# Routing that chooses tiles by halves, and a combination whose residual is laid out by rows

## The chip, the cores and the metric

The kernel runs on one core of a Trainium2 chip. The metric is device microseconds for one launch, lower is better; where several runs are shown, their median is given. Times inside an execution are counted from its first instruction.

## The reference, cut to what matters

The whole program is two layers on an image x of shape (2, 256, 64, 64): layer 0 is area attention and a recurrence over tokens, layer 1 is a convolution block with a selective scan and then a mixture of experts. The change touches only the mixture of experts, which is the last stage:

```python
t = _to_tokens(x)                       # 2 * 4096 tokens of 256 channels
t = t + _L1_ffn_ref(_ln_t(t), gate_w, gate_b, W1, b1, W2, b2)
x = _from_tokens(t, x)

def _ln_t(v, eps=1e-5):                 # over the 256 channels of a token
    return (v - mean(v)) / sqrt(var(v) + eps)

def _L1_ffn_ref(x, ...):                # 8 experts, hidden size 512
    probs = softmax(xf @ gate_w + gate_b)
    top2_vals, top2_idx = top_k(probs, 2)
    cw = zeros((N, 8)); cw[token, top2_idx] += top2_vals
    for each expert e:
        acc += cw[:, e, None] * (gelu(xf @ W1[e] + b1[e]) @ W2[e] + b2[e])
    return acc
```

## The kernel before

The stage is the function experts, and it has three parts that follow one another: route, run_blocks, combine. Inside route and run_blocks the instructions of each engine stand in the order in which the code names them; the five engines (PE for matrix products and transposes, DVE, ACT, POOL, and SP, which here only issues DMAs) meet through semaphores.

**Route.** There are 64 tiles of 128 tokens, and the loop in normalise takes four at a time, so g runs over 16 groups. The image lies in SBUF with tokens on partitions (tok, which is the tile sh.x). For each group, turn (L1721) transposes the eight 128x128 blocks on PE into a PSUM tile "turned" (three buffers of two banks each) and ACT copies them to x_turned (x in this function), which has channels on partitions. measure (L1728) takes statistics of each tile on DVE, one or two instructions a tile; centre_gate (L1707) takes the mean out of the gate weights. Each four groups, gates (L1761) multiplies the gate weights with those 16 tiles of x_turned on PE and copies the product out on DVE, and turn_gates (L1774) transposes it back by PE and puts the logits in place. The PSUM tile of the product, by_expert, has one buffer. After the loop, root (L1733) makes the factor inv and the offset less of every token: six DVE operations, a square root on ACT (with a table load) and two more on DVE. Then the last product is turned, and scale (L1747) normalises each group, three tiles on ACT and one on POOL, and SP stores the rows to DRAM (rows), from four buffers xt. Last, choose (L1799) finds the two best experts of each token on DVE with operations over all 64 tiles at once (128x512), and ACT takes the exponents.

What follows in route is not changed: ranks of the tokens within their expert, the block numbers (wi, for the weights), then a table of which token stands where, made of products of one-hot tiles (high and named, low; L1925 to L1937). high is placed in memory that the xt buffers held, and so waits for their stores. The index lists xi and ri at L1951 end it.

**Run_blocks.** 68 blocks of 256 token slots run as a pipeline: POOL gathers rows and weights by indirect DMA, PE turns (L1976) and multiplies (L1988, L1998), ACT takes the Gelu, DVE copies (L1978) and adds the offset (L2006), and POOL puts the results in DRAM by indirect DMA (L2013). Where a block index over 68 is needed, a conditional part follows.

**Combine.** 16 groups of 512 tokens. SP loads both results of each token (y, two tiles of 512 KB, four buffers each), ACT scales the first by its weight (L2068), DVE multiplies and adds the second (L2069), in four steps k; PE transposes each step's two halves into po (L2073). Token 4p + k stands in row p of step k, so the four steps' columns interleave in the output. po holds them one step after another, and the views at L2081 to L2083 interleave while reading: DVE adds the residual of the first half of the channels (L2085), ACT copies the second half out of PSUM (L2087) and POOL adds its residual (L2088), since POOL's operand is not in PSUM. The residual is x_turned, where the tokens of one image row are 128 elements apart. POOL issues the store (L2089).

Of the kernel before, what the change touches and what calls it, by code (L numbers as in the profile page):

```python
# [18 lines left out]
P = 128  # L19
# [1598 lines left out]
def experts(tc, sh, ap, out, half, left):  # L1618
# [19 lines left out]
    with ExitStack() as ctx:  # L1638
# [5 lines left out]

        x = cp.tile([P, 2, WW, P], F32, name="x_turned")


        gate = cp.tile([P, 2, 32], F32, name="gate")
        nc.gpsimd.memset(gate, 0.0)
# [36 lines left out]

        ex = cp.tile([P, TILES, E], F32, name="ex")
        best, total = (cp.tile([P, TILES], F32, name=n) for n in ("best", "total"))
        held = ctx.enter_context(ExitStack())
        wp = held.enter_context(tc.tile_pool(name="e_w", bufs=3))  # L1690
        weights_of = {}
        full = [P, TILES, E]

        def over_experts(t):
            return t.unsqueeze(2).to_broadcast(full)

        def over_tiles(t):
            return t.unsqueeze(1).to_broadcast(full)

        def normalise(p2, logits):  # L1700

            with ExitStack() as own:
                ps = own.enter_context(tc.tile_pool(name="e_psum_n", bufs=3, space=PSUM))
                pg = own.enter_context(tc.tile_pool(name="e_psum_g", bufs=1, space=PSUM))
                pn = own.enter_context(tc.tile_pool(name="e_n", bufs=2))

                def centre_gate():  # L1707
                    of_gate = pg.tile([P, 512], F32, name="by_expert")[:, :32]
                    for c in range(2):
                        nc.tensor.matmul(of_gate, sh.mean_w, gate[:, c], start=c == 0, stop=c == 1)  # L1710
                    for c in range(2):
                        nc.vector.tensor_tensor(gate[:, c], gate[:, c], of_gate, ALU.subtract)
# [17 lines left out]
                        for c in (0, 1) if t in left else (1,):  # L1730
                            nc.vector.bn_stats(half[:, t, c], tok[:, t, c * P : c * P + P])

                def root():  # L1733

                    records = half.rearrange("p t c (i k) -> p t (c i) k", k=3)
                    means = records[:, :, :, 1]
                    nc.vector.tensor_reduce(mean, means, AX.X, ALU.add)
                    nc.vector.tensor_scalar(mean, mean, 0.25, None, ALU.mult)
                    nc.vector.tensor_tensor(away, means, mean.unsqueeze(2).to_broadcast([P, TILES, 4]), ALU.subtract)
                    nc.vector.tensor_tensor(away, away, away, ALU.mult)  # L1740
                    nc.vector.scalar_tensor_tensor(away, away, 64.0, records[:, :, :, 2], ALU.mult, ALU.add)
                    nc.vector.tensor_reduce(var, away, AX.X, ALU.add)
                    nc.scalar.activation(inv, var, AF.Sqrt, scale=1.0 / C, bias=sh.eps5)
                    nc.vector.reciprocal(inv, inv)
                    nc.vector.scalar_tensor_tensor(less, mean, -1.0, inv, ALU.mult, ALU.mult)
# [14 lines left out]

                def gates(q):  # L1761

                    pe = pg.tile([P, TB], F32, name="by_expert")
                    for c in range(2):
                        for j in range(4):
                            nc.tensor.matmul(
                                pe[32 * j : 32 * j + 32], gate[:, c], x[:, c, group(4 * q + j)],
                                start=c == 0, stop=c == 1, tile_position=(0, 32 * j),
                            )
                    mine = pn.tile([P, TB], F32, name="by_expert_s", bufs=1)  # L1770
                    nc.vector.tensor_copy(mine, pe)
                    return q, mine
# [8 lines left out]
                    )  # L1781


                waiting = None
                for g in range(TILES // K):
                    turn(g)
                    measure(g)
                    if g == 4:
                        centre_gate()
                    if g > 4 and g % 4 == 1:  # L1790
                        waiting = gates(g // 4 - 1)
                    if g > 4 and g % 4 == 2:
                        turn_gates(*waiting)
                root()
                turn_gates(*gates(3))
                for g in range(TILES // K):
                    scale(g)

        def choose(p1, logits):  # L1799

            pr, left = (p1.tile(full, F32, name=n) for n in ("pr", "left"))
            of = p1.tile([P, TILES], F32, name="of")
            nc.vector.tensor_tensor(pr, logits, over_experts(inv), ALU.mult)
            nc.vector.tensor_tensor(pr, pr, over_tiles(gate_b), ALU.add)
            nc.vector.tensor_reduce(of, pr, AX.X, ALU.max)
            nc.vector.tensor_tensor(pr, pr, over_experts(of), ALU.subtract)
            nc.scalar.activation(one, going[:, 0, 0:1], AF.Exp)
            nc.scalar.activation(ex, pr, AF.Exp)
            picks = [p1.tile(full, F32, name=f"pick{i}") for i in range(2)]
            for i, pick in enumerate(picks):  # L1810
                shifted = pr
                if i == 1:

                    shifted = left
                    nc.vector.scalar_tensor_tensor(left, picks[0], -3e38, pr, ALU.mult, ALU.add)
                    nc.vector.tensor_reduce(best, left, AX.X, ALU.max)
                    nc.vector.tensor_tensor(left, left, over_experts(best), ALU.subtract)
                nc.vector.scalar_tensor_tensor(pick, shifted, 0.0, over_tiles(rank), ALU.is_equal, ALU.mult)
                first = p1.tile([P, TILES], F32, name=f"first{i}")
                nc.vector.tensor_reduce(first, pick, AX.X, ALU.max)  # L1820
                nc.vector.tensor_tensor(pick, pick, over_experts(first), ALU.is_equal)
            nc.scalar.activation(best, best, AF.Exp)
            return picks, left

        def weigh():
            nc.vector.tensor_reduce(total, ex, AX.X, ALU.add)
# [17 lines left out]
        def route():  # L1844
            with ExitStack() as own:
# [2 lines left out]
                shared = p1.tile([P, NBLK * E], F32, name="logits")  # L1848
                logits = shared[:, : TILES * E].rearrange("p (t e) -> p t e", e=E)
                own.enter_context(tc.manual_schedule())  # L1850
                with tc.tile_pool(name="e_n2", bufs=4) as p2:
                    normalise(p2, logits)
                picks, left = choose(p1, logits)
                p4 = own.enter_context(tc.tile_pool(name="e_r4", bufs=2))
                ps = own.enter_context(tc.tile_pool(name="e_psum_r", bufs=1, space=PSUM))

# [99 lines left out]
        def run_blocks(lo, hi):  # L1956
            with ExitStack() as own:
# [70 lines left out]
                for i in range(lo, hi):  # L2028
# [18 lines left out]
                    below = i, act, now[1]  # L2047
                    if i == 8:
                        weigh()
                for _ in down(*below, None):  # L2050
                    pass

        def combine():
            with ExitStack() as own:
                p2 = own.enter_context(tc.tile_pool(name="e_c2", bufs=3))
                p4 = own.enter_context(tc.tile_pool(name="e_c4", bufs=4))
                ps = own.enter_context(tc.tile_pool(name="e_psum_c", bufs=3, space=PSUM))
                for g in range(T // TB):
                    b, n0 = g * TB // N, g * TB % N
                    y = [p4.tile([P, K, C], F32, name=f"y{i}") for i in range(2)]  # L2060
                    for i in range(2):
                        at = i * T + g * TB
                        got = nc.sync.dma_start(y[i], results[at : at + TB].rearrange("(p k) d -> p k d", k=K))
                        for put in puts:
                            tc.add_manual_dep(got.ins, put, landed, reason="all results first")
                    po = ps.tile([P, 2, TB], F32, name="po")
                    for k in range(K):
                        nc.scalar.activation(y[0][:, k], y[0][:, k], AF.Copy, scale=by_row[:, g, k, 0:1])  # L2068
                        nc.vector.scalar_tensor_tensor(  # L2069
                            y[1][:, k], y[1][:, k], by_row[:, g, k, 1:2], y[0][:, k], ALU.mult, ALU.add  # L2070
                        )
                        for c in range(2):
                            nc.tensor.transpose(  # L2073
                                po[:, c, k * P : k * P + P], y[1][:, k, c * P : c * P + P], sh.ident
                            )
                    cut = slice(n0, n0 + TB)
                    res = p2.tile([P, 2, TB], F32, name="res")
                    r0, r1 = HH * b + n0 // WW, HH * b + (n0 + TB) // WW
                    for c in range(2):

                        to = res[:, c].rearrange("p (r q k) -> p r q k", q=WW // K, k=K)  # L2081
                        turned = po[:, c].rearrange("p (k r q) -> p r q k", k=K, q=WW // K)
                        before = x[:, c, :, r0:r1].rearrange("p (q k) r -> p r q k", k=K)  # L2083
                        if c == 0:
                            nc.vector.tensor_tensor(to, turned, before, ALU.add)  # L2085
                        else:
                            nc.scalar.copy(to, turned)  # L2087
                            nc.gpsimd.tensor_tensor(to, to, before, ALU.add)  # L2088
                    nc.gpsimd.dma_start(out[b, :, cut].rearrange("(c p) n -> p c n", p=P), res)  # L2089

        route()
        run_blocks(0, OFTEN)
# [139 lines left out]
```

## Time and profile before

| | us |
|---|---|
| median of 3 runs | 3119.97 |
| lowest and highest of them | 3113.37, 3124.25 |
| the profiled execution, its own time | 3109.25 |
| its span, first to last instruction | 3107.5 |
| first instruction of the routing on PE (L1725) | at 2383.4 |
| first gather of rows for a block (L1834) | at 2481.4 |
| first load of the combination (L2063) | at 3018.7 |
| last store of the combination issued (L2089) | at 3101.5 |

The profile is one execution. Its rows have the engine, the line of the code, the tile written and the tiles read, the shape and the count; a row of the timeline begins with the start and the length in us (several instructions merged have one length), and in brackets how long the engine had stood idle and what released it. "PEclk" is the TensorE clock that was granted, as a share of full speed, and the DMA share is the mean busy share of the core's 16 DMA engines.

### The profile page before, as it was taken

What the parts mean: (1) busy time and instruction counts of PE and PEld (TensorE: products, weight loads), DVE (VectorE), ACT (ScalarE), POOL (GpSimd) and SP (SyncE); (2) the same over time, 40 slices, a digit from 0 to 9 for tenths busy, and PEclk for the clock granted to TensorE, in tenths of its full rate; (3) what the DMA queues carried; (4) which work ended last, traced back from release to release, by engine and by line L of the source; (5) the groups of instructions that cost most, each with busy time, mean ns of one, the idle gap of its engine ahead of it and who ended that gap; (6) DMA issues with size and microseconds to landing.
All of it is one profiled execution on the core that took longest, in us unless ns stands there. A gap on an engine that the chain in (4) does not pass through costs nothing. (4 is left out here: it accounts for less than half of the span.)

```text
span 3107.5 us, 45476 instructions
## 1 busy us (share of the span) xinstructions
PE 2745.6 (88%) x17734; PEld 1510.5 (49%) x17734; DVE 2246.1 (72%) x3331; ACT 1356.0 (44%) x2433; POOL 1355.6 (44%) x1034
## 2 busy tenths in 40 slices
PE   6988999999999999998779999987888399999974
PEld 1222222222222222222159999973445378888862
DVE  5699999999999999998966666779887811111127
ACT  2334444444444444444434455557663722222223
POOL 0343454544445454444731200018773256666644
PEclk8998999999999999999889999999999789999995
DMA  3000000000000000000023000005552456666657
GB/s 123 1 1 1 1 1 1 1 1 1 1 1 1 1 1 1 1 1 1 1 69 144 35 1 1 1 12 139 142 150 64 159 178 224 227 232 224 223 192 275
DMA packets 58579, 220.34 MB, mean 71 GB/s; under 512 B 14424, under 2 KB 15328, under 8 KB 48624
## 3 DMA queue, kind: packets, MB, share of 16 engines
q0 software_dynamic: 25504, 125.50, 11.4%
q1 hardware_dynamic: 31616, 87.56, 8.9%
q10 hardware_dynamic: 1232, 4.25, 0.4%
q8 instruction: 142, 2.33, 0.3%
q14 instruction: 85, 0.70, 0.1%
HBM read 173.30 MB, written 43.58 MB: 70 GB/s over the span
## 5 line engine op out<-in xcount | busy, mean ns | idle before, releaser
L577 POOL TENSOR_TENSOR ex<-ex,ex 128x1024 f32<-128x1024 f32 x255 | 636.3, 2497 | 768.6 <-PE ps L266 752.4
L271 DVE TENSOR_REDUCE nm<-ps 128x2 f32<-128x1024 f32 x512 | 601.3, 1219 | 129.4 <-PE ps L266 128.9
L359 ACT ACTIVATE ex<-ps 128x1024 f32<-128x1024 f32 x512 | 496.9, 1021 | 363.3 <-PE ps L352 343.9
L320 DVE SCALAR_TENSOR_TENSOR acc<-vh,w_pe,acc 128x1008 f32<-128x1008 f32 (+7 forms) x384 | 561.3, 1464 | 7.1
L266 PE MATMUL ps<-k,q 32*128 32x512 f32 x2048 | 352.4, 665 | 14.1 <-DVE nm L271 14.1
L1978 DVE COPY xt<-px 128x512 f32<-128x512 f32 x68 | 47.0, 692 | 417.0 <-PE px L1976 408.6
L352 PE MATMUL ps<-q,k 32*128 32x512 f32 x2048 | 304.8, 632 | 0.0
L1990 ACT ACTIVATE act<-ph,wt 128x256 f32<-128x256 f32 x272 | 128.8, 474 | 398.6 <-PE ph L1988 376.6
L365 PE MATMUL av_o<-ex,vt 128*32 128x512 f32 x2048 | 295.2, 645 | 4.5 <-ACT ex L359 4.3
L1988 PE MATMUL ph<-xt,wt 128*128 128x256 f32 x1088 | 293.5, 393 | 5.3 <-DVE xt L1978 3.6
L1998 PE MATMUL py<-wt,act 128*128 128x256 f32 x1088 | 280.0, 381 | 0.0
L266 PEld LDWEIGHTS ps<-k,q 32*128 32x128 f32 x2048 | 120.9, 191 | 231.6 <-issue 83.6
L347 PE MATMUL ps<-mx,ones_b 3*128 3x512 bf16 x1024 | 139.9, 392 | 102.0 <-DVE nm L271 101.3
L1988 PEld LDWEIGHTS ph<-xt,wt 128*128 128x128 f32 x1088 | 191.8, 192 | 68.2 <-DVE xt L1978 25.6
L773 PE MATMUL z<-xs,u 128*128 128x128 f32 x1872 | 223.6, 276 | 0.0
L773 PEld LDWEIGHTS z<-xs,u 128*128 128x128 f32 x1872 | 217.1, 193 | 0.0
L1998 PEld LDWEIGHTS py<-wt,act 128*128 128x128 f32 x1088 | 202.7, 191 | 25.1
L797 ACT ACTIVATE t<-z,bias 128x128 f32<-128x128 f32 x468 | 136.3, 362 | 145.4 <-PE z L785 145.3
L2013 POOL DMA_INDIRECT results<-y,ri x136 | 134.3, 988 | 145.6 <-DVE y L2006 103.9
L347 PEld LDWEIGHTS <-ones_b 3*128 3x128 bf16 x1024 | 36.4, 91 | 310.0 <-issue 307.3
L785 PE MATMUL z<-xs,v 128*128 128x128 f32 x1512 | 179.6, 275 | 0.0
L785 PEld LDWEIGHTS z<-xs,v 128*128 128x128 f32 x1512 | 174.2, 192 | 0.2 <-DVE xs L804 0.2
(409 smaller groups left out, 3930.8 us busy)
## 6 DMA issues: line engine op xcount, KB each, us to landing
cs<-c_rows SPq DMA_DIRECT2D x128, 256.0 KB
y<-results SPq DMA_DIRECT2D x32, 512.0 KB
x<-xrows SPq DMA_DIRECT2D x8, 1024.0 KB
rows<-xt SPq DMA_DIRECT2D x16, 512.0 KB
out_x<-res POOLq DMA_DIRECT2D x16, 512.0 KB
xrows<-xn SPq DMA_DIRECT2D x24, 256.0 KB
x<-in_x SPq DMA_DIRECT2D x4, 1024.0 KB
x<-in_x ACTq DMA_DIRECT2D x4, 1024.0 KB
```

The costliest lines, as they stand in the source:

```text
L266: mm = nc.tensor.matmul(tiles[h // 2][:, h % 2], qs[G, i // HM][head(h), i % HM * P : (i % HM + 1) * P], ks[G, n][head(h)], start=True, st ...
L271: nc.vector.tensor_reduce(nms[G][:, n, 2 * j : 2 * j + 2, i], tiles[j], AX.X, ALU.max, negate=True)
L320: nc.vector.scalar_tensor_tensor(part, vh[:, c, 2 + r0 + dy : 2 + r1 + dy, w0 + dx : w1 + dx], w_pe[:, c, k : k + 1], part, ALU.mult, ALU.add,
L347: nc.tensor.matmul(tiles[h // 2][:, h % 2], ones_b[at], mxs[G, n][at], start=True, stop=False, tile_position=(HD * h, 0),)
L352: nc.tensor.matmul(tiles[h // 2][:, h % 2], k[head(h), m % HM * P : (m % HM + 1) * P], qs[G, n][head(h)], start=False, stop=True, tile_pos ...
L359: nc.scalar.activation(exs[i], tiles[i], AF.Exp, scale=HD**-0.5)
L365: nc.tensor.matmul(to[head(h)], lhs, exs[h // 2][:, h % 2], start=first, stop=last, tile_position=(0, HD * h))
L577: add = nc.gpsimd.tensor_tensor(pair[0], *pair, ALU.add)
L773: nc.tensor.matmul(z[c][:, g, :m], u[:, k, c, g], xt[:, k], start=g == GATES[0] and k == 0, stop=False, skip_group_check=True,)
L785: nc.tensor.matmul(z[c][:, g, :m], v[:, k, c, g], h[:, k], start=False, stop=k == 1, skip_group_check=True,)
L1988: nc.tensor.matmul(ph[:, hc], wt[:, at : at + P], xt[:, c], start=c == 0, stop=c == 1)
L1998: nc.tensor.matmul(py[:, j], act[:, hc, j * P : j * P + P], wt[:, at : at + C], start=hc == 0, stop=hc == NH - 1,)
```

## The change

Routing: the statistics of groups 0 to 7 are all taken at group 4 and those of groups 8 to 15 at group 5, followed at once by the first part of root. The gate product has two PSUM buffers and its copy out is a function of its own (take_gates); the turned tile has two buffers instead of three. The square root, and the choice for tiles 0 to 31, stand at group 10; from group 11 on, one group of scaling follows each turn. The last two gate products are turned after the loop, and the choice for tiles 32 to 63 comes after all scalings. The operations of choose are the same, on 128x256 each, so there are twice as many; the exponents stay whole.

Blocks: in blocks 12 to 43 DVE copies one piece of 128x512 of x_turned into the memory of sh.x, which nothing reads any more, in the order of the tokens (lay_out).

Combination: the transposes write po with a step of four elements, so that po is in the order of the tokens; DVE adds the residual of both halves in one instruction of 128x1024, ACT's copy and POOL's addition are gone, and y has five buffers. In the last group the halves are added and stored one by one, the second by SP.

```diff
...
+        placed = sh.x.rearrange("p c b n -> p (c b n)").rearrange("p (c m w) -> p c m w", c=2, w=WW)
...
-                ps = own.enter_context(tc.tile_pool(name="e_psum_n", bufs=3, space=PSUM))
+                ps = own.enter_context(tc.tile_pool(name="e_psum_n", bufs=2, space=PSUM))
...
-                def root():
+                def root_in():
...
                     nc.vector.tensor_reduce(var, away, AX.X, ALU.add)
+
+                def root_out():
+
                     nc.scalar.activation(inv, var, AF.Sqrt, scale=1.0 / C, bias=sh.eps5)
...
                 def gates(q):
 
-                    pe = pg.tile([P, TB], F32, name="by_expert")
+                    pe = pg.tile([P, TB], F32, name="by_expert", bufs=2)
...
+                    return q, pe
+
+                def take_gates(q, pe):
                     mine = pn.tile([P, TB], F32, name="by_expert_s", bufs=1)
                     nc.vector.tensor_copy(mine, pe)
                     return q, mine
...
                 for g in range(TILES // K):
                     turn(g)
-                    measure(g)
                     if g == 4:
+                        for i in range(8):
+                            measure(i)
                         centre_gate()
                     if g > 4 and g % 4 == 1:
                         waiting = gates(g // 4 - 1)
-                    if g > 4 and g % 4 == 2:
+                        if g < 12:
+                            waiting = take_gates(*waiting)
+                    if g == 5:
+                        for i in range(8, TILES // K):
+                            measure(i)
+                        root_in()
+                    if 4 < g < 12 and g % 4 == 2:
                         turn_gates(*waiting)
-                root()
-                turn_gates(*gates(3))
-                for g in range(TILES // K):
+                    if g == 10:
+                        root_out()
+                        halves[0]()
+                    if g > 10:
+                        scale(g - 11)
+                last = gates(3)
+                turn_gates(*take_gates(*waiting))
+                turn_gates(*take_gates(*last))
+                for g in range(5, TILES // K):
                     scale(g)
-
-        def choose(p1, logits):
...
+                halves[1]()
+
+        def choose(p1, logits, half):
+
+            at = slice(half * TILES // 2, (half + 1) * TILES // 2)
+            pr, left, *picks = (t[:, at] for t in p1)
...
+                    if 12 <= i < 12 + 2 * T // TB:
+                        lay_out(*divmod(i - 12, 2))
...
+        def lay_out(j, c):
+
+            rows_ = slice(j * TB // WW, (j + 1) * TB // WW)
+            nc.vector.tensor_copy(placed[:, c, rows_], x[:, c, :, rows_].rearrange("p w m -> p m w"))
...
-                p4 = own.enter_context(tc.tile_pool(name="e_c4", bufs=4))
+                p4 = own.enter_context(tc.tile_pool(name="e_c4", bufs=5))
...
-                    po = ps.tile([P, 2, TB], F32, name="po")
+
+                    po = ps.tile([P, 2, P, K], F32, name="po")
...
-                            nc.tensor.transpose(
-                                po[:, c, k * P : k * P + P], y[1][:, k, c * P : c * P + P], sh.ident
-                            )
+                            nc.tensor.transpose(po[:, c, :, k], y[1][:, k, c * P : c * P + P], sh.ident)
                     cut = slice(n0, n0 + TB)
                     res = p2.tile([P, 2, TB], F32, name="res")
-                    r0, r1 = HH * b + n0 // WW, HH * b + (n0 + TB) // WW
-                    for c in range(2):
-
-                        to = res[:, c].rearrange("p (r q k) -> p r q k", q=WW // K, k=K)
-                        turned = po[:, c].rearrange("p (k r q) -> p r q k", k=K, q=WW // K)
-                        before = x[:, c, :, r0:r1].rearrange("p (q k) r -> p r q k", k=K)
-                        if c == 0:
-                            nc.vector.tensor_tensor(to, turned, before, ALU.add)
-                        else:
-                            nc.scalar.copy(to, turned)
-                            nc.gpsimd.tensor_tensor(to, to, before, ALU.add)
-                    nc.gpsimd.dma_start(out[b, :, cut].rearrange("(c p) n -> p c n", p=P), res)
+                    before = placed[:, :, g * TB // WW : (g + 1) * TB // WW]
+                    parts = [slice(0, 2)] if g < T // TB - 1 else [slice(0, 1), slice(1, 2)]
+                    for eng, cs in zip((nc.gpsimd, nc.sync), parts):
+                        nc.vector.tensor_tensor(
+                            res[:, cs], po[:, cs].rearrange("p c m k -> p c (m k)"),
+                            before[:, cs].rearrange("p c m w -> p c (m w)"), ALU.add,
+                        )
+                        eng.dma_start(out[b, :, cut].rearrange("(c p) n -> p c n", p=P)[:, cs], res[:, cs])
```

## The prediction

> **What bounds the kernel now.** I read the page first, then the timeline of the two stages that the diff touches, then one stage's groups, and last the DMA shares by stretch. The page gives the stage map: DVE, ACT and DMA in 40 slices of 77.7 us.
>
> ```profile
> span 3107.5 us, 45476 instructions
> DVE  5699999999999999998966666779887811111127
> PEclk8998999999999999999889999999999789999995
> DMA  3000000000000000000023000005552456666657
> ```
>
> Routing lies in the 31st and 32nd slice, where DVE reads 7 and 8 (2383 to 2482 us); the run of 1 after it is the expert blocks, bound by PE; the last slice, where DVE is 7 and the granted clock 0.5, is the combination (3018.7 to 3107.5 us). The timeline of the combination shows its first group and a later one:
>
> ```profile
> 3023.87 1.67 DVE L2069 SCALAR_TENSOR_TENSOR y<-y,by_row,y 128x256 f32<-128x256 f32 x4 [10.23 <-DMA y<-results]
> 3026.41 1.01 DVE L2085 TENSOR_TENSOR res<-po,x_turned 128x512 f32<-128x512 f32 x1 [0.87 <-PE po L2073]
> ...
> 3045.42 1.01 DVE L2085 TENSOR_TENSOR res<-po,x_turned 128x512 f32<-128x512 f32 x1 [0.87 <-issue]
> 3046.34 2.99 DVE L2069 SCALAR_TENSOR_TENSOR y<-y,by_row,y 128x256 f32<-128x256 f32 x4
> ...
> 3047.14 1.52 POOL L2088 TENSOR_TENSOR res<-res,x_turned 128x512 f32<-128x512 f32 x1 [2.25 <-ACT res L2087]
> ...
> 3050.20 1.01 DVE L2085 TENSOR_TENSOR res<-po,x_turned 128x512 f32<-128x512 f32 x1 [0.87 <-issue]
> ```
>
> A group lasts 4.78 us (3045.42 to 3050.20). DVE is in it all the time: four multiply-adds, 0.87 waiting for PE's last transposes, one addition. The four take 1.67 in the first group, where POOL is idle, and 2.99 later; POOL's own addition of 1.52 starts inside them. The tile view of y shows where the 1.3 go: one in four is stretched.
>
> ```profile
> L2069 DVE SCALAR_TENSOR_TENSOR y<-y,by_row,y x64: 471/479/1811, 3023.9 to 3096.7; 128x256 f32<-128x256 f32 x64
> ```
>
> The page's chain of waits blames POOL; I read it as POOL lengthening DVE's round. Next the transfers of the stage: the column before the last is the DMA share, the last GB/s.
>
> ```profile
> 3030.00:3050.00 20.00, 9.91 (x36) 5.46 (x36) 15.97 (x21) 8.34 (x19) 9.75 (x9) 0.50 0.98 378
> 3070.00:3084.00 14.00, 6.69 (x24) 3.65 (x24) 11.39 (x16) 6.56 (x15) 6.72 (x6) 0.50 0.90 335
> 3084.00:3107.00 23.00, 6.69 (x24) 3.65 (x24) 12.40 (x16) 5.95 (x13) 8.96 (x8) 0.50 0.28 109
> ```
>
> The engines are full only while loads still run; the last 23 us carry stores alone at 0.28. Transfers are the next bound, not this one. Last the routing's timeline:
>
> ```profile
> 2413.71 0.35 ACT L1743 ACTIVATE inv<-var,eps 128x64 f32<-128x64 f32 x1
> 2414.94 23.69 ACT L1756 ACTIVATE xt<-x,less,inv 128x256 f32<-128x256 f32 x48 [0.88 <-DVE less L1745]
> 2416.40 0.29 DVE L1778 COPY logits<-by_token 128x128 f32<-128x128 f32 x1 [0.89 <-PE by_token L1777]
> 2426.93 0.69 DVE L1859 TENSOR_TENSOR both<-pick,pick 128x512 bf16<-128x512 f32 x1
> 2441.83 0.76 DVE L1925 TENSOR_TENSOR high<-place,hi 128x576 bf16<-128x576 bf16 x1 [1.68 <-DMA rows<-xt]
> ```
>
> Two chains meet at L1925: the normalised rows (root, 48 ACT scalings, their stores), and DVE's choice (logits, thirteen operations, the ranks), which is ready 1.68 us earlier. So routing ends on the row stores, with DVE 1.68 behind.
>
> **The change part by part: combination.** ACT's copy, POOL's addition and one of two DVE additions go; DVE adds both halves at once, 128x1024, from a PSUM tile and a residual that both lie in order. Durations:
> - The multiply-adds fall back to the first group's 1.67, as no POOL instruction reads SBUF beside them.
> - PE is then what the addition waits for: from the first multiply-add to the addition 3026.41 - 3023.87 = 2.54.
> - The addition: nearest rows are L1497 (DVE, 128x1024 out of PSUM) at 1.23 and L2006 at 0.69 for 512. I take 1.23; the next instruction starts 0.08 before its end, as now (3045.42 + 1.01 against 3046.34).
>
> So 2.54 + 1.15 = 3.69 a group. First multiply-add to last addition is 74.1 now (3023.9 to 3098.0); then 15 x 3.69 + 2.54 = 57.9: 16.2 less. The tail from the last addition to the end is 9.5 now (addition 1.0, ACT 0.6, POOL 1.5, gaps, then 6.0 from the issue at 3101.5). Then: two half additions 1.4, 0.1, and some 5.7 from SP's issue (0.32 instead of POOL's 0.73): 7.2, so 2.3 less. Combination: -18.5.
>
> Does the DMA allow it? 16 groups move 16 x 1.573 = 25.2 MB; at 390 GB/s (the best slice, 3020 to 3030) 4.0 us a group, above 3.69. But loads run ahead: at 390 GB/s the first five groups' loads (1.05 MB each) take 13.5 us without a store between them, one group more than the four buffers of now allow, and this lead of some three groups pays 16 x 0.3 = 5 us. So it just fits; the rival below is that it doesn't.
>
> **A rule against this step.** The transposes now write PSUM with a step of four elements, 16 bytes. The row: L1308 already writes with a step of two, and its 64-column matmul takes 216 ns where L1184's, written in order, takes 218. The Trainium skill, "SBUF — State Buffer", section "Door 1: The DMA port swizzle", says in its note on cachelines that PSUM has 8-byte lines and that any PSUM pattern out of order slows matmuls significantly. L1308 already meets a new line at each element, and pays nothing; so I add 0. By the rule it turns round. A group is 1.77 + 9x, with x the 0.213 us from one transpose to the next: 0.54 until the first (3024.41 in the trace), seven steps, 2x for the last, 0.08 to the addition, 1.15. With x doubled it is 5.6, and the combination gets 15 x 5.6 + 4.5 - 74.1 - 2.3 = 12 us longer instead of 18.5 shorter.
>
> **The residual's layout.** 32 DVE copies of 128x512, one a block in blocks 12 to 43, read with a step of 512 bytes. No row is the same: from 0.42 (L1740, 256 elements, if it runs at two a clock) to 1.52 (POOL on this very view); I take 1.0, like L2085. Each stands behind y's addition on DVE, and the next DVE instruction (the px copy L1978) comes after 5.99 us of idling in every block: 0 on the path. If that gap were gone, 32 us. POOL's queue of puts and gathers is the other neighbour; the trace has no SBUF-to-SBUF copy beside its indirect DMAs. The Trainium skill, same page, section "SBUF: two separate sides", says that such an fp32 copy keeps GpSimd from writing descriptors while it runs. By the trace POOL idles 1.47 before each block's put; by the rule the put starts later by the copy's length, and up to 1.5 that idling takes it. 0 by either.
>
> **Routing.** On DVE now: 32 measures of 0.198 from 2385.45 to 2391.8, gate centring to 2392.1 (0.9 later than before), idle 2.0 for the first gate product (1.92 on PE), its copy to 2394.8, then 46 measures and six root operations in one run: 9.1 + 2.7, to 2406.7 (before 2412.4). Behind that run stand the logits copy and the second gate copy; behind the latter PE's transposes of it, and behind these, on PE, the turns of groups 11 to 15. Before, all 16 turns were copied at 2408.9. Now PE stands from about 2401.5 to 2407.7. The root comes at 2408.4, 5.7 earlier, but ACT then alternates a copy (0.95) with three scalings (1.48): group 15's copy ends near 2410.2 + 4 x 2.43 = 2420. The 48 scalings end at 2437.7 against 2438.6, so the row stores gain only 1. The first half's choice (thirteen at 0.42 to 0.54, 6.3 with gaps) ends at 2415.7, hidden. But the last gate product needs group 15: it ends at 2422.0, and then transposes, copies, transposes and copy follow one another (2.65), then the second choice 6.3 and the sum 0.75: 2431.7 against 2427.6. DVE's slack of 1.68 is eaten and 2.4 remain. The two halves cost 12.6 for 10.2, which is part of this. A second bank for gate products saves nothing while ACT's copy decides; two turned buffers instead of three cost nothing, since ACT paces them. And the clock: it was granted 1.0 until 2415, 0.73 to 2417 and 0.5 after, some 5 us after PE fell idle, and needed as long to come back at 2383. PE's stand may cost that again; the last products then last up to 3.84. So +2 to +6.5; I take +3.5.
>
> **Sum.** -18.5 + 3.5 + 0 = -15.0. The profiled execution took 3109.25 (span 3107.5 and 1.75 around it): 3094.3. It lies 10.7 under the median of the runs shown, 3119.97; from that, 3105.0.
>
> **The rivals.**
> 1. Routing is no loss (0.17): if the clock holds and ACT's copies come between DVE's waits more kindly, the row stores still end it, 1 earlier. For: DVE has 1.68 to spare. Against: the last product behind ACT. -19: 3101.
> 2. Transfers become the bound (0.15): at the 378 GB/s of 3030 to 3050, 4.16 a group. 74.1 - (15 x 4.16 + 2.54) + 2.3 = 11.5 gained, 3.5 lost: 3112. For: share 0.98. Against: 0.28 at the end.
> 3. Slower (0.04): PSUM's step bounds PE. From x = 0.38 on, with 27.2 + 144x - 74.1 - 2.3 + 3.5, the total is over 0.3% slower; with x doubled it is 12 + 3.5 more: 3135.5. L1308 speaks against it.
> 4. It doesn't do what it says (0.04): the stretch of 1.3 is not POOL's and stays: 2.98 + 0.87 + 1.15 = 5.0 a group, +4 in all: 3124. Against: the first group.
>
> **How the numbers follow.** Likeliest (0.60): 3105. A measurement of this kernel can tell about 0.3%, 9.4 us; the three runs shown differ by 10.9. With some 4 us of spread around each case, the main one is faster by more than that at 0.92, rival 1 nearly always, rival 2 at 0.36, the others never: 0.77. Rival 3 and the far tails are slower: 0.06. Same: 0.17. Range: the routing's bounds, rival 1 below, rival 2 above, and the runs' spread: 3095 to 3115.
>
> **What would show it.** Right: no L2069 over 0.5 us, L2115 (the new addition) near 1.23 and 3.7 apart, no POOL addition, 128x128 transposes still 0.42; the copies beside blocks of unchanged 7.55; PE idle before by_token around 2402 to 2407, and high starting at 2444 to 2448 with no wait for the row stores. Wrong: transposes longer than 0.42, DVE waiting for y loads in the combination, or high before 2442.

## The result, and the profile after

The changed kernel takes 3100.19 us (median of 10 runs, 3094.54 to 3109.60); ten runs of the kernel before beside it have a median of 3118.18. The ratio is 0.9947, with a 95% interval of 0.9933 to 0.9961: faster by 12.2 to 20.9 us, by 18.0 between the medians. The forecast was 3105.0 with a range of 3095 to 3115.

The profiled execution of the changed kernel took 3105.5 us, only 3.75 less than that of before, and this pair of numbers would mislead. The two traces are best compared by stage, each from an instruction that both kernels have:

| stage | before | after | difference |
|---|---|---|---|
| start to the first turn of the routing (unchanged code) | 2383.5 | 2399.6 | +16.1 |
| routing, from the first turn to the first `high` | 58.4 | 62.0 | +3.6 |
| table and expert blocks, from `high` to the first y load | 576.9 | 571.7 | -5.2 |
| combination, from the first y load to the end | 88.7 | 70.3 | -18.4 |
| span | 3107.5 | 3103.5 | -4.0 |

The first and the third row are not the change's. In twelve executions of the kernels of this study the unchanged first stage ends anywhere between 2381.0 and 2399.6; most of the 16.1 arises in the attention before 1320 us. The third row comes from single late blocks among blocks of 7.55 us. In before the block after the second is 2.9 late, and one near the end is 2.4 late; in after neither is. The first lateness goes with the TensorE clock: in before full clock is granted again 62.9 after `high`, in after 56.5 after it, and in the ten executions where it comes at 61.1 to 62.9 this block is 2.0 to 2.9 late, in the two where it comes at 56.2 and 56.5 it is not. Why the second comes is not shown. Either turns up with the old routing and with the new. The two changed stages repeat better: the changed routing lies between 61.2 and 62.0 in five executions, the changed combination between 69.6 and 70.5 in six. So the experiments below are read by stages.

The page of after, the same rows as before:

```profile
span 3103.5 us, 45453 instructions
...
DVE  5689999999989999998966666779888832222115
...
PEclk8998999999999999999979999998999789999995
DMA  3000000000000000000012200004553336666658
```

In the last slice DVE has gone from 7 to 5 and the DMA engines from 7 to 8: less work for DVE, and the same bytes in a shorter time. The timeline of the combination after, one group and the start of the next:

```profile
3045.71 1.66 DVE L2105 SCALAR_TENSOR_TENSOR y<-y,by_row,y 128x256 f32<-128x256 f32 x4
...
3046.24 1.97 PE L2109 MATMUL po<-ident,y 128*128 128x128 f32 x8 [1.71 <-DVE y L2105]
3048.25 1.23 DVE L2115 TENSOR_TENSOR res<-po,x 128x1024 f32<-128x1024 f32 x1 [0.87 <-PE po L2109]
3049.39 1.66 DVE L2105 SCALAR_TENSOR_TENSOR y<-y,by_row,y 128x256 f32<-128x256 f32 x4
...
3051.94 1.23 DVE L2115 TENSOR_TENSOR res<-po,x 128x1024 f32<-128x1024 f32 x1 [0.89 <-PE po L2109]
```

A group lasts 3051.94 - 3048.25 = 3.69 us, and the four multiply-adds 1.66. The tile view of y (minimum, median and maximum in ns) shows that none is stretched any more:

```profile
L2105 DVE SCALAR_TENSOR_TENSOR y<-y,by_row,y x64: 474/479/486, 3038.3 to 3095.7; 128x256 f32<-128x256 f32 x64
```

The transfers in the middle of the stage (the third column from the right is the granted clock, then come the DMA share and GB/s):

```profile
3057.00:3069.00 12.00, 6.38 (x27) 4.68 (x28) 9.32 (x18) 5.18 (x13) 2.90 (x4) 0.50 1.03 419
```

The engines are full, at 419 GB/s. DVE waits for a load inside the stage only once, for 0.45.

The routing after, on PE, DVE and ACT:

```profile
2416.60 1.09 PE L1729 MATMUL turned<-ident,x 128*128 128x128 f32 x8
2423.51 1.12 PE L1787 MATMUL by_token<-ident,by_expert_s 128*128 128x128 f32 x4 [5.81 <-DVE by_expert_s L1781]
2424.42 5.17 PE L1729 MATMUL turned<-ident,x 128*128 128x128 f32 x24
...
2435.91 1.00 ACT L1730 COPY x_turned<-turned 128x1024 f32<-128x1024 f32 x1
...
2439.49 0.29 DVE L1788 COPY logits<-by_token 128x128 f32<-128x128 f32 x1 [7.04 <-PE by_token L1787]
...
2448.12 0.77 DVE L1887 TENSOR_TENSOR both<-pick,pick 128x512 bf16<-128x512 f32 x1
...
2461.56 0.81 DVE L1953 TENSOR_TENSOR high<-place,hi 128x576 bf16<-128x576 bf16 x1 [0.23 <-issue]
```

PE stands for 5.81 us behind the copy of the second gate product. The turns that follow take 5.17 for 24, against 2.78 before, since the granted clock had fallen to 0.5. The row of before, and the stretch of after with its clock (third column from the right):

```profile
2400.91 2.78 PE L1725 MATMUL turned<-ident,x 128*128 128x128 f32 x24
```

```profile
2423.00:2427.00 4.00, 3.49 (x17) 3.49 (x18) 2.69 (x7) 1.99 (x3) 1.15 (x2) 0.50 0.02 4
```

ACT's last copy starts at 2435.91, DVE waits 7.04 for the last but one gate product, and `high` no longer waits for the row stores: DVE's own chain now ends the routing.

### The profile page after: what moved, and what is told of

Same layout as the page of the kernel before. It is cut to its first block, busy times and chain, and to the rows that moved or that the text cites. A ratio compares the mean times of both kernels' runs of the same rounds, so it can differ in the third digit from the quotient of the medians.

```text
span 3103.5 us, 45453 instructions
## 1 busy us (share of the span) xinstructions
PE 2755.1 (89%) x17734; PEld 1515.8 (49%) x17734; DVE 2253.2 (73%) x3377; ACT 1348.7 (43%) x2417; POOL 1332.3 (43%) x1018
## 5 line engine op out<-in xcount | busy, mean ns | idle before, releaser
L2006 DVE COPY xt<-px 128x512 f32<-128x512 f32 x68 | 47.0, 692 | 395.1 <-PE px L2004 395.1
L2016 PEld LDWEIGHTS ph<-xt,wt 128*128 128x128 f32 x1088 | 190.4, 191 | 65.8 <-DVE xt L2006 23.5
```

What stands on the lines that cost most here:

```text
L2016: nc.tensor.matmul(ph[:, hc], wt[:, at : at + P], xt[:, c], start=c == 0, stop=c == 1)
```

## The experiments

All times that follow are us from the profile of the kernel named; "both", "copy of group 15" and "high" are starts counted from the first turn. Each stage length is that of one execution. The measured stages together:

| kernel | both | copy of group 15 | high | combination |
|---|---|---|---|---|
| before | 43.5 | 24.5 | 58.4 | 88.7 |
| after | 48.5 | 36.3 | 62.0 | 70.3 |
| combination alone | 42.3 | 23.3 | 57.2 | 70.5 |
| routing alone | 48.0 | 36.1 | 61.5 | 89.2 |
| no GpSimd addition | 42.5 | 23.5 | 57.4 | 77.0 |
| GpSimd addition beside | 48.0 | 36.1 | 61.3 | 83.7 |
| po in order | 48.0 | 36.1 | 61.2 | 71.4 |
| four y buffers | 48.0 | 36.0 | 61.5 | 69.6 |
| scalings behind | 44.8 | 32.7 | 60.5 | 69.6 |
| second copy earlier | 49.0 | 37.1 | 62.5 | 69.8 |
| gates turned late | 44.1 | 24.8 | 57.5 | 70.5 |
| root before the last copies | 41.1 | 25.3 | 54.6 | 70.3 |

**The two parts alone.** The kernel before with the new `combine` (its five y buffers too), `lay_out` and its calls; the calls are

```diff
...
+                    if 12 <= i < 12 + 2 * T // TB:
+                        lay_out(*divmod(i - 12, 2))
...
```

> The kernel before with the new combination, the layout copies and five y buffers, and with the old routing. Stage lengths in the profile: routing from the first turn to high 58.4 before and 62.0 after; combination from the first y load to the end 88.8 and 70.3. Theory (the two parts are independent; the combination gains 18.5 and the routing loses 3.6): routing 58.4, combination 70.3, the time before less 18.5, so a ratio of 0.994. Rival (the routing only loses because the layout or the fifth buffer moves something, or the combination gains from an earlier end of the routing): routing 60 or more, or a combination of 72 or more.

The median is 3096.09 us against 3116.51, a ratio of 0.9935 (0.9923 to 0.9948). The routing is 57.2 and the combination 70.5: the gain needs nothing of the new routing. And the changed routing with the old combination, without the layout copies:

> The changed routing with the old combination and without the layout copies. Theory: routing 62.0, combination 88.8, so 3.6 more than before, with the stretched multiply-adds (one in four at 1.81) back. Rival (part of the routing's 3.6 is scatter between executions): routing 58 to 60. The blocks between high and the first y load were 576.9 before and 571.7 after: if that belongs to the routing, they take some 572 here and some 577 with the old routing; if it is scatter (the clock's return in the first two blocks, and one block that is 2.4 late), it follows neither.

`high` comes at 61.5 and the combination takes 89.2, with multiply-adds of up to 1.81 again. The blocks take 574.2 here and 573.9 with the combination alone, so the 5.2 of the third stage follow neither part. Five executions with the changed routing as it is (after, routing alone, GpSimd addition beside, po in order, four y buffers) have `high` at 61.2 to 62.0, mean 61.5; three with the old one at 57.2 to 58.4, mean 57.6. The routing's loss is 3.9.

**GpSimd's addition taken away, and put back.** (GpSimd is POOL in the rows, VectorE is DVE, ScalarE is ACT, TensorE is PE.) First it goes from the kernel before, and ScalarE's copy with it; VectorE adds both halves:

```diff
-                        if c == 0:
-                            nc.vector.tensor_tensor(to, turned, before, ALU.add)
-                        else:
-                            nc.scalar.copy(to, turned)
-                            nc.gpsimd.tensor_tensor(to, to, before, ALU.add)
+                        nc.vector.tensor_tensor(to, turned, before, ALU.add)
```

> The kernel before, whose combination adds both halves of a group on VectorE (two additions of 128x512 as they stand); ScalarE's copy and GpSimd's addition are gone, everything else stays. Theory (GpSimd's addition is what stretches one multiply-add in four to 1.81): no multiply-add over 0.5, four in 1.67; a group is 1.67 + 0.87 + 2 x 0.93 = 4.40 against 4.78, and the combination 88.8 less 15 x 0.38 less 1 to 2 at the end: 81 to 82. Rival (the stretch comes from the y loads or from ScalarE): four multiply-adds still take 2.99, a group 2.99 + 0.87 + 1.86 = 5.7, and the combination about 102.

The combination takes 77.0, less than expected. Its timeline, of an early and of a later group:

```profile
3031.67 1.97 PE L2073 MATMUL po<-ident,y 128*128 128x128 f32 x8 [2.43 <-DVE y L2069]
...
3033.68 1.96 DVE L2084 TENSOR_TENSOR res<-po,x_turned 128x512 f32<-128x512 f32 x2 [0.87 <-PE po L2073]
...
3052.71 1.66 DVE L2069 SCALAR_TENSOR_TENSOR y<-y,by_row,y 128x256 f32<-128x256 f32 x4
...
3053.24 1.97 PE L2073 MATMUL po<-ident,y 128*128 128x128 f32 x8 [2.01 <-DVE y L2069]
3054.82 1.94 DVE L2084 TENSOR_TENSOR res<-po,x_turned 128x512 f32<-128x512 f32 x2 [0.45 <-PE po L2073]
...
3056.70 1.65 DVE L2069 SCALAR_TENSOR_TENSOR y<-y,by_row,y 128x256 f32<-128x256 f32 x4
```

The multiply-adds are at 1.66 though the additions still are the old ones, so the stretch came from what was taken away, GpSimd's addition or ScalarE's copy; the next run tells which. The first four groups take 4.40, as expected. From the fifth on a group takes some 3.98: the first addition then waits 0.45 for PE and not 0.87. In the early group it starts when all eight transposes are done (3031.67 + 1.97 = 3033.64), in the later one 0.39 before that (3053.24 + 1.97 = 3055.21). Eleven groups shorter by 0.42 are 4.6, which is what the forecast of 81 to 82 lacked; why only the later groups need not wait for all eight is not shown. Of the combination's 18.4, the move of GpSimd's addition to VectorE brings 11.7. The rest, 77.0 - 70.3 = 6.7, comes with the residual and PSUM in order, one addition a group, and the last group stored in halves; these were not taken apart.

Then the converse: the changed kernel, with a GpSimd addition of the old size in each group, on which nothing waits (`idle` is a tile of its own).

```diff
...
+                idle = p2.tile([P, TB], F32, name="idle", bufs=1)
...
+                    nc.gpsimd.tensor_tensor(
+                        idle.rearrange("p (r q k) -> p r q k", q=WW // K, k=K),
+                        idle.rearrange("p (r q k) -> p r q k", q=WW // K, k=K),
+                        x[:, 1, :, r0:r1].rearrange("p (q k) r -> p r q k", k=K), ALU.add,
+                    )
...
```

> The changed kernel with GpSimd adding, once a group, the old strided 128x512 view of the residual to a tile of its own that nobody reads: an addition of the old size beside the multiply-adds, on which nothing waits. Theory (it is this that stretches one multiply-add in four): one in four at 1.8, a group 2.99 + 0.87 + 1.15 = 5.0 against 3.69, the combination 70.3 + 15 x 1.3 = 90. Rival (the stretch needs the old chain, in which GpSimd's addition waited on ScalarE's copy): multiply-adds at 0.48, a combination of 70 to 72.

It takes 83.7, neither 90 nor 70. The order of GpSimd's work is why: with nothing to wait for, its sixteen additions run in one row from the stage's start.

```profile
3027.94 26.20 POOL L2113 TENSOR_TENSOR idle<-idle,x_turned 128x512 f32<-128x512 f32 x16
...
3039.84 6.33 DVE L2107 SCALAR_TENSOR_TENSOR y<-y,by_row,y 128x256 f32<-128x256 f32 x4
3046.95 1.22 DVE L2123 TENSOR_TENSOR res<-po,x 128x1024 f32<-128x1024 f32 x1 [0.78 <-PE po L2111]
3048.10 6.33 DVE L2107 SCALAR_TENSOR_TENSOR y<-y,by_row,y 128x256 f32<-128x256 f32 x4
...
3056.35 1.66 DVE L2107 SCALAR_TENSOR_TENSOR y<-y,by_row,y 128x256 f32<-128x256 f32 x4
```

While they run, four multiply-adds take 6.33; the next four, after GpSimd's end at 3054.1, take 1.66. Eleven of the 64 are stretched, to 1.33 to 1.74, and DVE's multiply-adds take 39.8 in all against 26.7 in the changed kernel. The 13.1 between them are all but the whole lengthening of 13.4. ScalarE's copy of the old chain is in neither kernel, so GpSimd's addition alone stretches. DVE's own addition, which reads PSUM and one SBUF operand, takes its usual 1.22 in the middle of this.

**The order in PSUM.** The changed kernel with the transposes written in order; the rival here is the rule that the prediction cites.

```diff
-                    po = ps.tile([P, 2, P, K], F32, name="po")
+                    po = ps.tile([P, 2, K, P], F32, name="po")
...
-                            nc.tensor.transpose(po[:, c, :, k], y[1][:, k, c * P : c * P + P], sh.ident)
+                            nc.tensor.transpose(po[:, c, k], y[1][:, k, c * P : c * P + P], sh.ident)
...
-                        nc.vector.tensor_tensor(
-                            res[:, cs], po[:, cs].rearrange("p c m k -> p c (m k)"),
-                            before[:, cs].rearrange("p c m w -> p c (m w)"), ALU.add,
-                        )
+                        for c in range(cs.start, cs.stop):
+                            nc.vector.tensor_tensor(
+                                res[:, c].rearrange("p (m k) -> p m k", k=K), po[:, c].rearrange("p k m -> p m k"),
+                                before[:, c].rearrange("p m w -> p (m w)").rearrange("p (m k) -> p m k", k=K), ALU.add,
+                            )
```

> The changed kernel with the transposes written to PSUM in order (runs of 512 bytes) instead of with a step of 16 bytes; VectorE reads them with a step of 512 bytes, in two additions of 128x512, against a residual and a result that lie in order. Theory (the step of 16 bytes costs TensorE nothing): transposes 0.42, eight in 1.94 to 1.97, as with the step. Rival (the rule that PSUM out of order slows matmuls): eight take under 1.8 here. What the additions take tells which operand made the old ones slow: 1.01, as in the kernel before, if it was PSUM's step (then a group is 1.66 + 0.45 + 1.93 = 4.0 and the combination 75 to 77); 0.7 if it was the residual's (a group 3.4 to 3.7, and the combination 66 to 71, if the transfers allow it).

The tile views of y, of this kernel (L2109 there too) and of the changed one:

```profile
L2109 PE MATMUL po<-ident,y x128: 418/421/477, 3030.9 to 3089.5; 128*128 128x128 f32 x128
```

```profile
L2109 PE MATMUL po<-ident,y x128: 417/421/477, 3038.9 to 3096.6; 128*128 128x128 f32 x128
```

The step of 16 bytes costs PE nothing, at the granted clock of 0.5 that both have here; no run has these transposes at full clock. The additions, by this kernel's timeline:

```profile
3062.86 0.48 DVE L2105 SCALAR_TENSOR_TENSOR y<-y,by_row,y 128x256 f32<-128x256 f32 x1 [1.19 <-DMA y<-results]
3063.26 1.28 DVE L2116 TENSOR_TENSOR res<-po,x 128x512 f32<-128x512 f32 x2
```

Two take 1.28, though they read PSUM with a step of 512 bytes: the old 1.01 apiece came with the residual's view, not with PSUM's step. A group could be shorter than 3.69 now, but the combination takes 71.4: DVE waits for y loads, with the DMA engines at a share of 1.02 to 1.03. Less work on DVE no longer helps this stage.

**Four y buffers.** One number changed in the changed kernel:

```diff
-                p4 = own.enter_context(tc.tile_pool(name="e_c4", bufs=5))
+                p4 = own.enter_context(tc.tile_pool(name="e_c4", bufs=4))
```

> The changed kernel with four buffers for y instead of five. In the changed kernel the DMA engines are full through the middle of the combination (share 1.03 at 419 GB/s), a group's loads land every 3.74 us, and VectorE waits for a load once, 0.45. Theory (the lead of the fifth buffer is what lets 3.69 a group run against full transfers): VectorE waits for loads in several groups and the combination takes 72 to 74.5 instead of 70.3. Rival (the transfers carry 3.69 without it): 70.3 within 0.3.

The rival holds: 69.6, as short as the shortest of the changed combination, and no wait for a load after the first. DVE's waits for loads in the combination, in us in all, times, longest:

```profile
DVE y L2105 <- DMA y<-results: 10.1, 1, 10.1
```

**The routing's loss, taken apart.** Two causes lie one behind the other: PE stands until the second gate product is copied, and ACT's last five copies stand behind the root and alternate with scalings. One experiment takes away each. First the interleaving:

```diff
-                    if g > 10:
-                        scale(g - 11)
...
-                for g in range(5, TILES // K):
+                for g in range(TILES // K):
                     scale(g)
```

> The changed kernel with one thing undone: ScalarE's scalings come behind all its copies instead of three after each copy from group 11 on. TensorE's stand behind the run of measures stays. The changed kernel has group 15's copy at 36.3 after the first turn, both at 48.5 and high at 62.0 with 0.2 of waiting. Theory (stand first, interleaving second): group 15's copy at 34, both at 44.7, but the scalings now end at 58.4, so high waits some 3 us for the row stores and comes at 61.6: nothing gained. Rival (the interleaving alone makes the loss): high at 58 or earlier.

Both starts at 44.8, as expected, and then `high` waits for the row stores, at 60.5:

```profile
2458.18 0.76 DVE L1951 TENSOR_TENSOR high<-place,hi 128x576 bf16<-128x576 bf16 x1 [2.29 <-DMA rows<-xt]
```

Then the order on DVE:

```diff
                     if g == 5:
-                        for i in range(8, TILES // K):
+                        for i in range(8, 12):
+                            measure(i)
+                    if g == 9:
+                        for i in range(12, TILES // K):
                             measure(i)
                         root_in()
```

> The changed kernel with the copy of the second gate product ahead of the last measures (groups 12 to 15) instead of behind all of them; the interleaved scalings and the square root ahead of the copies of groups 11 to 15 stay. Theory (the copies of groups 11 to 15 wait on ScalarE for the root as well, so freeing TensorE alone is worth little): group 15's copy at 35 to 36, both at 47 to 48, high at 61 to 62. Rival (TensorE's stand of 6 us and the half clock after it are the whole loss): both at 45 or earlier, high at 58 to 59.

Nothing is gained, as expected: `high` at 62.5. PE turns two more groups (11 and 12) and then stands all the same, now 8.72 for ACT, whose copy of group 11 is behind the root:

```profile
2409.54 1.97 PE L1729 MATMUL turned<-ident,x 128*128 128x128 f32 x8 [8.72 <-ACT x_turned L1730]
```

So both have to go together. This kernel takes both away in the changed one:

```diff
-                    if 4 < g < 12 and g % 4 == 2:
+                    if g == 6:
                         turn_gates(*waiting)
-                    if g == 10:
-                        root_out()
-                        halves[0]()
-                    if g > 10:
-                        scale(g - 11)
+                    if g == 9:
+                        second = waiting
+                root_out()
+                turn_gates(*second)
                 last = gates(3)
-                turn_gates(*take_gates(*waiting))
+                third = take_gates(*waiting)
+                halves[0]()
+                turn_gates(*third)
                 turn_gates(*take_gates(*last))
-                for g in range(5, TILES // K):
+                for g in range(TILES // K):
                     scale(g)
```

> The changed kernel with its routing mended: the second gate product is turned on TensorE behind the last of the 16 turns, the square root comes behind the last copy on ScalarE, and the 48 scalings come behind all copies. Theory (the routing loses since TensorE stands behind the long run of measures and ScalarE's last copies then alternate with scalings): TensorE has no gap of over 2 us before the gates' transposes, both starts 42.7 after the first turn (48.5 in the changed kernel, 43.5 before), high at 56.1 with no wait for the row stores (62.0 and 58.4): the time 5.9 under the changed kernel's and 20.8 under that of before, a ratio of 0.9933. Rival (the loss is the price of choosing by halves, twice thirteen operations, and of the measures ahead of everything): both at 47 or later, high at 60 to 62.

The copies end as early as before (24.8), the loss of the routing is gone (57.5), but it gains nothing on the old routing, and both comes 1.4 later than expected. DVE stands for the square root, which is now behind all 16 copies:

```profile
2413.71 0.55 DVE L1751 RECIPROCAL inv<-inv 128x64 f32<-128x64 f32 x1 [3.80 <-ACT inv L1750]
```

The median is 3097.01, the ratio 0.9932 (0.9914 to 0.9949). The last step moves the root ahead of the copies of groups 14 and 15 (the edit is against the kernel just shown):

```diff
                     if g == 9:
                         second = waiting
-                root_out()
+                    if g == 13:
+                        root_out()
```

> The last kernel with the mended routing (gates turned late), with the square root moved ahead of ScalarE's copies of groups 14 and 15. There VectorE stood 3.80 us for the square root, behind copies and the loading of ScalarE's table (1.28), and high came at 57.5. Theory (that stand is what the mended routing still loses): the root is out 2.4 earlier, both starts at 41.7 (44.1 there) and high at 55.1 with no wait for the row stores; combination 70.5. The time is then 2.4 under that kernel's, which the stage lengths can show and the medians cannot. Rival (the delayed copies of groups 14 and 15 hold the last gate product back by as much): both at 44, high at 57 to 58.

Both starts at 41.1 and `high` at 54.6, a little earlier than expected; `high` is ready when DVE is:

```profile
2415.76 0.55 DVE L1751 RECIPROCAL inv<-inv 128x64 f32<-128x64 f32 x1 [0.95 <-ACT inv L1750]
...
2432.28 0.69 DVE L1889 TENSOR_TENSOR both<-pick,pick 128x512 bf16<-128x512 f32 x1
...
2445.82 0.81 DVE L1955 TENSOR_TENSOR high<-place,hi 128x576 bf16<-128x576 bf16 x1 [0.23 <-issue]
```

By its stages this is the best kernel: 6.9 shorter in the routing than the mean of the changed one, 3.0 than the old, with the same combination. It still chooses by halves, so the halves are not what lost. Its median of 3096.0, ratio 0.9938 (0.9924 to 0.9952), can't be told from the other two kernels timed here, nor surely from the changed one: the unchanged first stage alone spreads over 18.6 us.

## Why the prediction was right, point by point

- **The combination's sum held.** A group of 3.69 was forecast and measured, and for the stage -18.5 against -18.4. First multiply-add to last addition was put at 57.9 and is 58.7 (3097.04 - 3038.34), since one group waits 0.45 for a load and later ones take up to 3.79; in "scalings behind", where DVE waits for no load inside the stage, it is 57.9. The tail was put at 7.2 and is 6.5. That these two misses cancel is luck.
- **The cause held.** No multiply-add is over 0.49, and taking GpSimd's addition away or putting it back takes and brings the stretch. Rival 4 falls.
- **PSUM's step cost 0**, as L1308's row had said, and not what the Trainium skill's rule on PSUM out of order ("SBUF — State Buffer", "Door 1: The DMA port swizzle") would have made of it: 421 ns with the step and without, both at half clock. Rival 3 falls.
- **The residual's layout was free, but its copy was mis-sized**: 0.59 instead of 1.0, within the bounds of 0.42 to 1.52. The blocks stay at 7.55, and their stage takes 573.9 with the copies (combination alone) and 574.0 without (no GpSimd addition). GpSimd's put beside such a copy takes 1.10 against 0.99 before and starts no later after y, so the rule in the section "SBUF: two separate sides", on descriptors held back, shows as 0.1 at most, and that hidden. Whether this copy, which reads with a step, is of the kind that the section means, no run here shows.
- **The transfers were mis-sized.** The step "at 390 GB/s 4.0 us a group", from a slice early in the stage, led to a lead of 5 us that only the fifth buffer would give. Early in the stage (3045 to 3057) full engines move 399 GB/s after the change too, later 419; why they differ is not shown. At 419 a group's 1.573 MB takes 3.75, almost DVE's 3.69; four buffers do as well. Rival 2's 378 was not what the engines could give, and it falls, though one of the named signs of being wrong, DVE waiting for a y load, shows once, for 0.45. It was right that transfers are next: with po in order they are the bound.
- **The routing held almost step by step.** PE's stand was put at 18.0 to 24.2 after the first turn, and lies at 18.1 to 23.9; the root was put 5.7 earlier, and is 5.8. The working then left a loss of 2.4, and 3.5 was taken because the half clock after the stand was left open; the loss is 3.6 in the profiled execution and 3.9 as a mean. The half clock came. With it eight turns take 1.95 (2426.37 - 2424.42) and not 1.09, so ACT's copy of group 11 ends at 27.8 after the first turn and not at 26.7, and `both` ends at 49.3 and not at 48.2. The row stores' gain of 1 shrank by the same delay: the scalings end at 55.0, against 54.2 in the forecast and 55.2 before. So the steps were right, but that 3.5 came so near is in part luck: its last 1.1 had no working. Rival 1 (no loss) falls: ACT's copies did not come more kindly.
- **The total.** -15.0 was forecast and -18.0 measured, with an interval of -12.2 to -20.9 that holds both; by the stages it is -18.4 + 3.9 = -14.5. The 3.0 between have no place in the stages, and are not explained further. Another 1.8 of the 4.8 between 3105.0 and 3100.19 is that ten runs of before have a lower median than the first three, 3118.18 and not 3119.97.

## What to carry to other kernels

Ask of an operation moved to GpSimd what runs beside it on VectorE: here an addition of 1.5 us on GpSimd cost each group 1.3 us of VectorE's time, and VectorE does it itself in 1.0. When a long run of one engine's work is pulled ahead, look up what stands behind it on every queue; here two queues blocked the same product one behind the other, and undoing either alone gained 1.0 us or nothing. Measure a small change by the stage it sits in, between two instructions that both kernels have, when untouched stages scatter by more than it is worth.

## What the runs showed of the hardware

- A multiply-add with two SBUF operands and a GpSimd addition out of SBUF hold each other up. In the kernel before, one of each begins together:

```profile
3047.13 1.80 DVE L2069 SCALAR_TENSOR_TENSOR y<-y,by_row,y 128x256 f32<-128x256 f32 x1
3047.14 1.52 POOL L2088 TENSOR_TENSOR res<-res,x_turned 128x512 f32<-128x512 f32 x1 [2.25 <-ACT res L2087]
```

  The multiply-add, 0.48 when alone, ends 0.27 after GpSimd's addition. Nearly all of the loss is VectorE's: with the addition put beside, one of GpSimd's takes 1.51 before the first multiply-add and up to 1.59 among them. Where GpSimd's additions follow in a row, the two take turns, one to one: a multiply-add takes up to 1.74, and one of GpSimd's begins every 1.64 (26.2 / 16). An addition with one operand in PSUM runs beside GpSimd at its usual 1.22. The section "SBUF: two separate sides" of the Trainium skill's "SBUF — State Buffer" calls this an exclusive lock on a shared port, for VectorE operations with two SBUF inputs against a GpSimd operation that reads SBUF; the numbers here agree.
- DVE read PSUM with a step of 512 bytes at no cost: 0.68 for 128x512, like 0.69 in order (L2006 of before). The old addition of that size took 1.01, with the residual read out of order in SBUF. A plain copy that reads the residual with a step of 512 bytes takes 0.59, so the step alone is not the reason, which stays open.
